# GNN attention over sorted edges: 132 groups of edges summed by counting in place of 120, four in every batch

## The chip, the core and the metric

The kernel runs on one core of a Trainium2 chip. The metric is the device time of one execution in microseconds; the median of three runs of the kernel before is 3422.3 us (3422.07 to 3423.4).

## The reference, cut to what matters

One attention layer of a graph network over 12,500 nodes and 400,000 edges with 64 features each, then a residual and a layer norm. The edges are sorted by destination, and the destinations are drawn as 12500·u², so low nodes have many edges and high nodes few.

```python
z_att = jnp.concatenate([h_src, h_dst, efeats], axis=-1)      # h_src = x[src], h_dst = x[dst]
e = leaky_relu(z_att @ W_attn + b_attn)[:, 0]
m = jnp.concatenate([h_src, efeats], axis=-1) @ W_ne
alpha = softmax of e over the edges of one destination        # segment max, exp, segment sum
z = segment_sum(alpha[:, None] * m, dst)
out = relu(concatenate([x, z]) @ W_out)
return layernorm(x + out)
```

## The kernel before

**Groups and batches.** 512 edges make a group (128 partitions by T = 4); there are 782 groups in the order of the destinations. The first `DG` = 120 groups are *dense*: few nodes receive all their edges. The other 662 are gathered: they go through the main loop in batches of up to 16 groups (`sizes`, from `starts`), in four parts of up to four groups (`lots`); the last four batches have the sizes given by `ENDS` (10, 10, 12 and 6). That makes 43 batches, numbered from 0.

**A gathered group.** GpSimd (POOL) fetches the source rows with four indirect DMAs a group (`gather`, L348, 128 rows of 65 floats each, from `table` to `zx`), 64 for a batch of 16. `scores` (L383 to L409) computes the scores of one part on VectorE (DVE): products and sums with the edge features (L390, L392), the addition of the gathered term (L397, which waits for the part's gathers), the one-hot of the destinations and its sums (L399 to L408). When the four parts of a batch are scored, `softmax` runs on the batch (L721 is its first instruction), then `weights` (L818), and TensorE (PE) multiplies `zx` by the weights (`products`, L835): two parts right after the softmax, two inside the next batch's softmax. `add_in` (L852) adds the sums into `acc`, a ring of 2048 columns with 48 spare columns at its end, which `unwrap` folds back.

**A dense group** needs no gather. Its source terms are looked up by one-hot products (`look_turn`, `look_products`, L470, and `look_scores`, L495 to L501). Rounds of 12 dense groups (`ROUNDS`) join the softmax of a batch. Then `dense_counts` builds, per group, one-hots of source block and node on ScalarE (ACT; L509, L510 and, for nodes above `FIT` = 5, L522, L523), weighted one-hots `lows` on DVE (L512), and multiplies them on PE into a PSUM bank (L517) and, for the sixth and seventh node of a group, into two columns shared by all groups (`more_nodes`, L525). `dense_sum` adds these into `counts` (L535, L538). At the end of a *chunk* of dense groups (`CHUNKS`) `node_products` multiplies `counts` with all of x (L594, 50 instructions on PE), `node_pick` takes the result and clears `counts` (L602, L605, L607), `node_turn` and `node_sum` add it to the sums. `NODS` says how many nodes a group of a given number may span, `EACHS` how many dense groups a batch takes (four below group 84, three from there).

**The order** of instructions is written out by hand for PE, DVE, ACT, SP and POOL (`tc.manual_schedule`): each engine runs what the loop issues, in the loop's order. Per batch, over the parts i = 0 to 3: scores of part i; at i = 0 `node_products` of a chunk that the batch before has closed, then the products with the edges' features (L578), and, after a chunk, `finish3` of a block of nodes that is complete (L1093 to L1109); at i = 1 the first look-up, the first dense group's counts and `between` (`far` on ACT, L664, and on DVE L668, which waits for it); at i = 2 the look-ups' edge scores (L480 to L489) and, only where a batch has four, the second group's counts. Inside the softmax `dense_step(n)`, n = 0 to 3, does `node_pick` (n = 0), the look-ups' scores, `dense_sum`, and the remaining counts (n = 2, 3):

```python
if n == 0 and opened:
    opened = node_pick(*opened)
...
if n in (0, 3):
    while open_counts:
        dense_sum(*open_counts.pop(0))
```

Gathers are kept in step with PE: a gather at a place of a batch waits for a PE instruction (`marks`, `STEPS`), and single-element matmuls (`look_at`, L339) wait on PE for gathers to land; a gather four places on waits for each of them.

The counts' one-hots and the look-ups' share six buffers (`big`, `BIG` = 6). In the batches with looks, the one-hot for the sixth node is written to a buffer that the first look-up's product (L470) must have read.

In the kernel before, chunks from group 84 on have six groups, two batches of three; so every second of these batches has a chunk's `node_products`.

Of the kernel before, what the change touches and what calls it, by code (L numbers as in the profile page):

```python
# [25 lines left out]
S = 48  # L26
# [6 lines left out]
HQ = 4  # L33
EW = 65
ZB = 8
ROUNDS = (12, 12, 12, 12, 12, 12, 12, 12, 12, 12)
DB = len(ROUNDS)
EACHS = ((84, 4), (120, 3))
EACH = max(n for _, n in EACHS)
CHUNKS = ((36, 1), (12, 2), (8, 3), (6, 6))  # L40
NODS = ((16, 2), (36, 3), (60, 4), (87, 5), (108, 6), (120, 7))
FIT = 5
ND = 32
HC = 4
# [3 lines left out]
RING = 2048  # L48
# [10 lines left out]
BF16 = mybir.dt.bfloat16  # L59
# [4 lines left out]
def sorted_path(ctx, tc, x, dst, idx, edge, w_ne, w_attn, b_attn, w_out, out, flag):  # L64
# [6 lines left out]
    nc = tc.nc  # L71
# [19 lines left out]
    ones_col = const.tile([P, 1], F32, name="ones_col")  # L91
    nc.vector.memset(ones_col, 1.0)

    ENDS = ((3, 3, 2, 2), (3, 3, 2, 2), (3, 3, 3, 3), (2, 2, 1, 1))
    sizes = [sum(parts) for parts in ENDS]
    DG = sum(ROUNDS)
    BD = max(ROUNDS)
# [19 lines left out]
    def nodes_of(g):  # L117
        return next(n for upto, n in NODS if g < upto)

# [24 lines left out]
    acc = const.tile([P, RING + S], F32, name="acc")  # L144
# [6 lines left out]
    wins = [dram.tile([P, S], F32, name=f"wins{k}") for k in range((NG + P - 1) // P)]  # L151
# [279 lines left out]
    def look_loads(g0, n):  # L431

        many = nodes_of(g0)
        wrow = tiny.tile([P, EACH, NOD], F32, name="wrow_d", bufs=1)[:, :, 0:many]
        nc.sync.dma_start(out=wrow[:, 0:n], in_=wins[0][g0:g0 + n, 0:many].unsqueeze(0).to_broadcast([P, n, many]))
        return dense_edges(g0, n, "ed", True), wrow

    def look_row(g):
# [89 lines left out]
    def dense_sum(g, to):  # L528

        _, vs = nc.values_load_multi_w_load_instructions(  # L530
            rel[0:1, g:g + 1], engines=(EngineType.DVE,), min_val=0, max_val=ND - nodes_of(g),
            skip_runtime_bounds_check_because=within)
        n = min(FIT, nodes_of(g))
        at = counts[:, :, ds(vs[0], n)]
        nc.vector.tensor_tensor(at, at, to.rearrange("p (h n) -> p h n", n=n), op=OP.add)  # L535
# [62 lines left out]
    def node_pick(g0, pairs):  # L598

        pr = feats.tile([P, SG, T, D], F32, name="pr", bufs=1)  # L600
        mine = pr[:, 0]
        nc.vector.tensor_tensor(mine, pairs[:, 0:HC * D].rearrange("p (h f) -> p h f", f=D),  # L602
                                own.unsqueeze(2).to_broadcast([P, HC, D]), op=OP.mult)
        sums_ = work.tile([P, D], F32, name="sums_", bufs=1)
        nc.vector.tensor_reduce(sums_, mine.rearrange("p h f -> p f h"), axis=AX.X, op=OP.add)  # L605
        if g0 + chunk_sizes[-1] < DG:
            nc.vector.memset(counts, 0.0)  # L607
        return g0, sums_
# [233 lines left out]
    def add_in(g0, n, pg, b0, fac):  # L842
        Sk = widths[starts.index(b0)]
        _, vs = nc.values_load_multi_w_load_instructions(
            column[b0][0:1, g0 - b0:g0 - b0 + n], engines=(EngineType.DVE,), min_val=0, max_val=RING - 1,
            skip_runtime_bounds_check_because=within)
        for g in range(n):
            if g == 0 and fac is not None:
                a1 = acc[:, ds(vs[0], 1)]
                nc.vector.tensor_scalar(a1, a1, fac, None, op0=OP.mult)  # L850
            ag = acc[:, ds(vs[g], Sk)]
            nc.vector.tensor_tensor(ag, ag, pg[:, g, :], op=OP.add)  # L852
# [36 lines left out]
    ids = pre.tile([DG, P, 2 * T], I32, name="ids", bufs=1)  # L889
    nc.sync.dma_start(out=ids, in_=idx[0:DG])  # L890
# [10 lines left out]
    with before:  # L901
# [23 lines left out]
        with tc.manual_schedule(engines={EngineType.DVE, EngineType.Pool, EngineType.Activation, EngineType.PE, EngineType.SP}):  # L925
# [59 lines left out]
            parted_row = pre.tile([DG, P, T], I32, name="parted_row", bufs=1)  # L985
            nc.vector.tensor_scalar(parted_row, ids[:, :, 0:T], P - 1, None, op0=OP.bitwise_and)
            low_row = pre.tile([DG, P, T], BF16, name="low_row", bufs=1)
            nc.scalar.activation(low_row, parted_row, AF.Copy)
            nc.sync.dma_start(out=low_rows, in_=low_row)
# [136 lines left out]
    with loop:  # L1126
# [55 lines left out]
        with tc.manual_schedule(engines={EngineType.PE, EngineType.DVE, EngineType.Activation, EngineType.SP, EngineType.Pool}):  # L1182
# [13 lines left out]
            for k, G in enumerate(sizes):  # L1196
# [22 lines left out]
                for i, (g0, n) in enumerate(lots[k]):  # L1219
# [628 lines left out]
```

## Time and profile before

| | |
|---|---|
| median of three runs | 3422.3 us |
| the profiled execution | 3425.55 us, span 3423.7 us |
| granted TensorE clock, mean | 0.683 |
| busy, share of the span | POOL 73%, PE 67%, DVE 62%, ACT 38% |
| gathers from `table` (L348) | 2584 |
| matmuls of `products` (L835) | 5152, 1059.7 us busy |
| `node_products` (L594) | 600 in 12 chunks, 157.8 us busy |

Busy shares are means over the span; POOL's does not count the time in which it issues. In the text a *lap* is the time from the softmax's first instruction (L721) of one batch to that of the next. A lap has a softmax half (L721 to the first L390 of the next batch's scores) and a scores half (from there to the next L721).

### The profile page before, as it was taken

Reading aid. Unit: us, or ns where it says so; the run is one execution under the profiler, and the core shown is the slowest. Engines: PE = TensorE matmul, PEld = TensorE weight load, DVE = VectorE, ACT = ScalarE, POOL = GpSimd, SP = SyncE. Lnnn points to the kernel's source line nnn. Section 1 sums busy time; section 2 is a strip of 40 time slices with the busy share of each in tenths; the row PEclk is TensorE's granted clock in tenths of the full one; section 3 lists DMA queues with packets and bytes.
Section 4 is the critical chain, followed back from the end, with each engine's and each line's share of the span. In section 5 each row is a group of like instructions: output and inputs, shape, how many; then the busy total and the mean of one; then the engine's idle time right before and its main releaser. Section 6 shows DMA issues by size and latency. Waiting matters only on the chain. (4 is left out here: it accounts for less than half of the span.)

```text
span 3423.7 us, 39637 instructions
## 1 busy us (share of the span) xinstructions
PE 2283.8 (67%) x10338; PEld 1912.0 (56%) x10338; DVE 2121.2 (62%) x5433; ACT 1292.3 (38%) x2838; POOL 2513.9 (73%) x2676
## 2 busy tenths in 40 slices
PE   0244456676677687786878787766767677776844
PEld 0144456666566575665657565655656565554743
DVE  5644455566666676666666666756667675656665
ACT  0211123343343344344444444234444444444321
POOL 6777777777777777777777777777777777777672
PEclk9999995555555566666666676656666676776655
DMA  9433333333333343333333333333333333333231
GB/s 127 87 67 67 67 73 76 74 75 74 78 77 82 75 84 78 85 76 77 79 75 76 71 73 72 77 70 75 75 73 78 71 64 71 66 69 61 46 69 21
DMA packets 518237, 250.75 MB, mean 73 GB/s; under 512 B 354395, under 2 KB 475578, under 8 KB 518003
## 3 DMA queue, kind: packets, MB, share of 16 engines
q1 hardware_dynamic: 429756, 159.38, 20.2%
q0 software_dynamic: 84960, 88.33, 16.4%
q8 instruction: 87, 1.43, 0.2%
q10 hardware_dynamic: 3286, 0.40, 0.2%
q14 instruction: 148, 1.20, 0.1%
HBM read 241.09 MB, written 6.79 MB: 72 GB/s over the span
## 5 line engine op out<-in xcount | busy, mean ns | idle before, releaser
L348 POOL DMA_INDIRECT zx<-table,srcs x2584 | 2443.5, 946 | 826.4 <-issue 697.4
L835 PE MATMUL pg<-w,zx 128*128 128x16 f32 (+9 forms) x5152 | 1059.7, 378 | 14.4 <-DVE w L818 11.9
L835 PEld LDWEIGHTS pg<-w,zx 128*128 128x128 f32 x5152 | 1041.9, 312 | 35.0 <-DVE w L818 13.8
L517 PE MATMUL pg<-big,lows 128*128 128x490 f32 (+3 forms) x960 | 498.0, 682 | 226.0 <-DVE lows L512 223.5
L517 PEld LDWEIGHTS pg<-big,lows 128*128 128x128 f32 x960 | 246.2, 271 | 418.0 <-issue 312.1
L509 ACT ACTIVATE big<-places,place 128x490 f32<-128x490 int16 (+3 forms) x480 | 293.8, 612 | 34.5 <-PE pg L470 33.7
L339 PE MATMUL pps<-zx,ident 1*1 1x1 f32 x272 | 24.4, 159 | 421.2 <-DMA zx<-table,srcs 421.2
L392 DVE TENSOR_REDUCE fixed<-pr 128x16 f32<-128x1024 f32 (+3 forms) x172 | 204.2, 1187 | 162.8 <-ACT fixed L387 154.0
L625 PE MATMUL lines<-ident,bnd 128*1 128x128 f32 x172 | 52.0, 405 | 318.2 <-ACT bnd L728 299.3
L510 ACT ACTIVATE big<-big 128x490 f32<-128x490 f32 (+3 forms) x480 | 257.1, 536 | 15.3
L339 PEld LDWEIGHTS pps<-zx,ident 1*1 1x1 f32 x272 | 10.9, 76 | 448.9 <-DMA zx<-table,srcs 388.6
L470 PE MATMUL pg<-s_src,big 128*128 128x98 f32 x960 | 256.9, 447 | 0.2 <-ACT big L452 0.2
L397 DVE TENSOR_TENSOR fixed<-fixed,zx 128x16 f32<-128x16 f32 (+3 forms) x172 | 31.7, 184 | 363.7 <-DMA zx<-table,srcs 359.3
L470 PEld LDWEIGHTS pg<-s_src,big 128*128 128x128 f32 x960 | 235.4, 329 | 0.9 <-ACT big L452 0.3
L390 DVE TENSOR_TENSOR pr<-ze,lines 128x1024 f32<-128x1024 f32 (+3 forms) x172 | 201.5, 1172 | 8.9 <-DMA ze<-in_edge_dram 8.7
L387 ACT ACTIVATE fixed<-wrow 128x96 f32<-128x96 f32 (+11 forms) x172 | 44.8, 261 | 419.9 <-DVE w L818 143.3
L625 PEld LDWEIGHTS lines<-ident,bnd 128*1 128x1 f32 x172 | 12.8, 97 | 324.8 <-ACT bnd L728 314.1
L723 ACT ACTIVATE soft<-turned 128x128 f32<-128x128 f32 x43 | 16.7, 389 | 459.0 <-DVE turned L721 459.0
L497 DVE TENSOR_TENSOR pr<-pr,pg 128x392 f32<-128x392 f32 x120 | 67.5, 562 | 196.7 <-PE pg L470 195.2
L388 ACT ACTIVATE zx<-ze 128x1024 f32<-128x1024 f32 (+3 forms) x172 | 176.5, 1026 | 11.2 <-DMA zx<-table,srcs 2.3
L852 DVE TENSOR_TENSOR acc<-acc,pg 128x16 f32 (+9 forms) x662 | 123.0, 186 | 77.9 <-issue 19.6
L512 DVE TENSOR_SCALAR lows<-fixed,low,kept 128x128 f32<-128x128 f32 x480 | 163.7, 401 | 8.0 <-PE pg L517 7.6
(305 smaller groups left out, 3010.1 us busy)
## 6 DMA issues: line engine op xcount, KB each, us to landing
ze<-in_edge_dram SPq DMA_DIRECT2D x326, 256.0 KB
zx<-table,srcs POOLq DMA_INDIRECT x2584
low_of<-low_rows SPq DMA_DIRECT2D x120, 128.0 KB
ep<-in_edge_dram SPq DMA_DIRECT2D x120, 128.0 KB
ed<-in_edge_dram SPq DMA_DIRECT2D x54, 256.0 KB
table<-xall SPq DMA_DIRECT2D x7, 455.0 KB
out_dram<-yo SPq DMA_DIRECT2D x24, 128.0 KB
xall<-in_x_dram SPq DMA_DIRECT2D x13, 224.0 KB
```

The costliest lines, as they stand in the source:

```text
L348: issued.append(nc.gpsimd.indirect_dma_start(out=zx[0:r, g, t, 1:EW] if plain else zx[0:r, g, t, 0:EW], out_offset=None, in_=x[:, :] if pl ...
L388: nc.scalar.activation(zx[0:r, 0:n, :, EW:EW + D], ze[0:r, 0:n], AF.Copy)
L390: nc.vector.tensor_tensor(pr[0:r, 0:n], ze[0:r, 0:n], w_edge[0:r].unsqueeze(1).to_broadcast([r, n, T, D]), op=OP.mult)
L392: nc.vector.tensor_reduce(ysum[0:r, 0:n], pr[0:r, 0:n], axis=AX.X, op=OP.add)
L470: at_hand[0] = nc.tensor.matmul(found[:, t, :], hot[:, :, t], s_src, start=True, stop=True).ins
L497: nc.vector.tensor_tensor(hits, hits, found, op=OP.mult)
L509: nc.scalar.activation(hi, places[:, 0:wide], AF.Square, bias=place[:, t, g:g + 1])
L510: nc.scalar.activation(hi, hi, AF.Relu, scale=-1.0, bias=1.0)
L512: nc.vector.tensor_scalar(lows[t], count_, low[:, t, g:g + 1], kept[:, t, kept_at(g):kept_at(g) + 1], op0=OP.is_equal, op1=OP.mult)
L517: at_hand[0] = nc.tensor.matmul(to, lows[t], highs[t], start=(t == 0), stop=(t == T - 1)).ins
L835: at_hand[0] = nc.tensor.matmul(pg[:, g, :], zx[:, g, t, 1:EW + D], w[:, g, t, :], start=(t == 0), stop=(t == T - 1)).ins
L852: nc.vector.tensor_tensor(ag, ag, pg[:, g, :], op=OP.add)
```

## The change

`DG` grows from 120 to 132 (eleven rounds of 12), so 12 groups leave the main loop: 650 groups are gathered, in 42 batches, the last four of 12, 12, 12 and 6. Every batch takes four dense groups. From group 84 on, a chunk is four groups, so that each of these batches closes a chunk; groups from 84 to 107 may span six nodes, those to 131 seven. `node_pick` moves from the softmax's first step to just ahead of the scores of the third part, for all chunks; where the batch's groups span more than five nodes, `dense_sum` of the first group stands behind it, so that the second group's counts find the shared columns free. In `add_in` the ring's spare columns are folded once per batch. Some loads at the start are made in two pieces, since 132 groups exceed 128 partitions.

```diff
-ROUNDS = (12, 12, 12, 12, 12, 12, 12, 12, 12, 12)
+ROUNDS = (12, 12, 12, 12, 12, 12, 12, 12, 12, 12, 12)
-EACHS = ((84, 4), (120, 3))
+EACHS = ((132, 4),)
-CHUNKS = ((36, 1), (12, 2), (8, 3), (6, 6))
-NODS = ((16, 2), (36, 3), (60, 4), (87, 5), (108, 6), (120, 7))
+CHUNKS = ((36, 1), (12, 2), (8, 3), (4, 12))
+NODS = ((16, 2), (36, 3), (60, 4), (84, 5), (108, 6), (132, 7))
...
-    ENDS = ((3, 3, 2, 2), (3, 3, 2, 2), (3, 3, 3, 3), (2, 2, 1, 1))
+    ENDS = ((3, 3, 3, 3), (3, 3, 3, 3), (3, 3, 3, 3), (2, 2, 1, 1))
...
             if g == 0 and fac is not None:
+                nc.vector.tensor_tensor(acc[:, 0:S], acc[:, 0:S], acc[:, RING:RING + S], op=OP.add)
+                nc.vector.memset(acc[:, RING:RING + S], 0.0)
                 a1 = acc[:, ds(vs[0], 1)]
...
+                    if i == 2 and opened:
+                        opened = node_pick(*opened)
+                    if i == 2 and batch_counts and nodes_of(batch_counts[0]) > FIT:
+                        while open_counts:
+                            dense_sum(*open_counts.pop(0))
                     hot = scores(g0, n, tiles[i], drel, b0, k == 0)
...
-                    if n == 0 and opened:
-                        opened = node_pick(*opened)
```

On DVE, in the scores half of the lap that ends with the softmax of batch 29 (a batch with a chunk and with groups of six nodes), ahead of the third part's scores. Before (`far` is what L668 waits for; L390 is the third part's first instruction):

```order
L512 TENSOR_SCALAR lows<-fixed,low,kept 128x128 x4
L668 ISA step,ups<-far 128x129
L668 ISA ups 128x1
L390 TENSOR_TENSOR pr<-ze,lines 128x1024
L392 TENSOR_REDUCE fixed<-pr 128x16
```

And in the changed kernel at the same place:

```order
L512 TENSOR_SCALAR lows<-fixed,low,kept 128x128 x4
L668 ISA step,ups<-far 128x129
L668 ISA ups 128x1
L602 TENSOR_TENSOR pr<-pg,own 128x256
L605 TENSOR_REDUCE sums__17881<-pr 128x64
L607 MEMSET counts 128x3136
L530 TENSOR_LOAD rel
L535 ISA
L535 TENSOR_TENSOR counts<-counts,pg 128x98x5
L538 ISA
L538 TENSOR_TENSOR counts<-counts,pps 128x98
L390 TENSOR_TENSOR pr<-ze,lines 128x1024
```

The chunk's pick and the first group's sums now stand between `far` and the third part's scores.

On PE in the same batch, from `node_products` (L594) to the softmax's first product (L625). Before:

```order
L594 MATMUL pg<-xall,counts 128x256 x24
L594 MATMUL pg<-xall,counts 64x128
L578 MATMUL pg<-wd,ep 128x12 x6
L470 MATMUL pg<-s_src,big 128x98 x4
L517 MATMUL pg<-big,lows 128x490 x4
L525 MATMUL pps<-big,lows 128x98 x4
L339 MATMUL pps<-zx,ident 1x1 x2
L625 MATMUL lines<-ident,bnd 1x4x32 x2
```

And in the changed kernel:

```order
L594 MATMUL pg<-xall,counts 128x256 x24
L594 MATMUL pg<-xall,counts 64x128
L578 MATMUL pg<-wd,ep 128x12 x8
L470 MATMUL pg<-s_src,big 128x98 x4
L517 MATMUL pg<-big,lows 128x490 x4
L525 MATMUL pps<-big,lows 128x98 x4
L517 MATMUL pg<-big,lows 128x490 x4
L525 MATMUL pps<-big,lows 128x98 x4
L339 MATMUL pps<-zx,ident 1x1 x2
L625 MATMUL lines<-ident,bnd 1x4x32 x2
```

A second group's counts (L517, L525) now stand ahead of the two matmuls that wait for gathers, and the products with the edges' features have eight instructions in place of six. This sequence comes in each of batches 26 to 33 (with looks) and, without L470, in batches 34 to 37; before it came in every second one of these batches.

More of the change, by code (lines that the diff above doesn't have):

```diff
@@ L434, in look_loads @@
         wrow = tiny.tile([P, EACH, NOD], F32, name="wrow_d", bufs=1)[:, :, 0:many]
-        nc.sync.dma_start(out=wrow[:, 0:n], in_=wins[0][g0:g0 + n, 0:many].unsqueeze(0).to_broadcast([P, n, many]))
+        nc.sync.dma_start(out=wrow[:, 0:n], in_=wins[g0 // P][g0 % P:g0 % P + n, 0:many].unsqueeze(0).to_broadcast([P, n, many]))
         return dense_edges(g0, n, "ed", True), wrow
@@ L888, in sorted_path @@
     lists[1] = listed(1)
-    ids = pre.tile([DG, P, 2 * T], I32, name="ids", bufs=1)
-    nc.sync.dma_start(out=ids, in_=idx[0:DG])
+    ids = [pre.tile([min(P, DG - a), P, 2 * T], I32, name="ids", bufs=1 + (DG - 1) // P) for a in range(0, DG, P)]
+    for a, part in zip(range(0, DG, P), ids):
+        nc.sync.dma_start(out=part, in_=idx[a:min(a + P, DG)])
     nc.sync.dma_start(out=meet, in_=dst[DG * GE - 1:DG * GE + 1].unsqueeze(0))
@@ L984, in sorted_path @@
             nc.scalar.activation(count_, places[:, 0:P], AF.Copy)
[L985 to L989, printed above, removed]
+            for a, part in zip(range(0, DG, P), ids):
+                n = min(P, DG - a)
+                parted_row = pre.tile([P, P, T], I32, name="parted_row", bufs=1)[0:n]
+                nc.vector.tensor_scalar(parted_row, part[:, :, 0:T], P - 1, None, op0=OP.bitwise_and)
+                low_row = pre.tile([P, P, T], BF16, name="low_row", bufs=1)[0:n]
+                nc.scalar.activation(low_row, parted_row, AF.Copy)
+                nc.sync.dma_start(out=low_rows[a:a + n], in_=low_row)
             of_dense = dense_list()
```

## The prediction

> **What bounds the kernel now.** I read first the groups of instructions and POOL's own line. (Columns of the first row: busy us, mean ns | idle before; of the second: duration min/median/max, first and last start.)
>
> ```profile
> L348 POOL DMA_INDIRECT zx<-table,srcs x2584 | 2443.5, 946 | 826.4 <-issue 697.4 <-DMA zx<-table,srcs 41.5 <-PE pps L339 25.7
> ...
> L348 POOL DMA_INDIRECT zx<-table,srcs x2584: 862/945/3402, 101.0 to 3369.8; - x199
> ```
>
> From 101.0 to 3369.8 us POOL does nothing but gather: 2584 gathers in 3268.8 us, and nearly all of its idle time is called issue, that is, it waited for nothing. Then I cut the time into laps, from one softmax's start to the next, and into stretches of laps. (Columns: length, then busy us and instructions of PE, PEld, DVE, ACT and POOL, then the granted clock.)
>
> ```profile
> 1793.80:1873.80 80.00, 70.14 (x297) 55.64 (x297) 54.11 (x139) 39.11 (x76) 60.48 (x65) 0.71 0.38 79
> 2113.60:2765.70 652.10, 462.29 (x2120) 381.24 (x2120) 423.58 (x1025) 269.70 (x568) 486.43 (x515) 0.65 0.35 73
> 2353.80:2436.60 82.80, 62.86 (x301) 52.16 (x301) 52.53 (x130) 37.74 (x79) 62.68 (x67) 0.73 0.34 72
> 2436.60:2517.50 80.90, 56.31 (x261) 46.08 (x261) 57.11 (x135) 38.02 (x81) 58.69 (x63) 0.63 0.37 76
> 2765.70:3088.50 322.80, 232.99 (x1102) 187.62 (x1102) 203.28 (x492) 150.25 (x340) 239.98 (x254) 0.67 0.33 66
> 3088.50:3345.70 257.20, 164.98 (x806) 140.02 (x806) 155.40 (x403) 94.99 (x225) 181.15 (x192) 0.61 0.30 59
> ```
>
> A lap of 64 gathers takes 80.0 us where nothing else interferes (first row), so a gather costs 80.0 / 64 = 1.25 us. No other engine is near full. But the lap 2353.80 to 2436.60 takes 82.8: it scores a batch with a chunk of six-node groups. Its DVE tells why.
>
> ```profile
> 2391.66 1.22 DVE L390 TENSOR_TENSOR pr<-ze,lines 128x1024 f32<-128x1024 f32 x1
> ...
> 2412.38 1.36 DVE L512 TENSOR_SCALAR lows<-fixed,low,kept 128x128 f32<-128x128 f32 x4
> 2422.54 0.29 DVE L668 CUSTOM_DVE_ANT_0 step<-far 128x129 f32<-128x129 f32 x1 [8.81 <-ACT far L664]
> ...
> 2422.76 1.21 DVE L390 TENSOR_TENSOR pr<-ze,lines 128x1024 f32<-128x1024 f32 x1
> ...
> 2433.80 0.19 DVE L397 TENSOR_TENSOR fixed<-fixed,zx 128x16 f32<-128x16 f32 x1
> ...
> 2436.61 0.32 DVE L721 STREAM_TRANSPOSE turned<-soft 128x128 f32<-128x128 f32 x1
> ```
>
> DVE idles 8.81 us ahead of the third part, for `far` on ACT. At 2433.80 L397, which waits for the part's gathers, does not wait at all: here the gathers are not the bound, the chain PE, ACT, DVE is. The two engines ahead of it:
>
> ```profile
> 2403.27 13.68 PE L594 MATMUL pg<-xall,counts 128*128 128x256 f32 x50 [4.17 <-DVE earlies L1275]
> 2416.88 1.51 PE L578 MATMUL pg<-wd,ep 128*128 128x12 f32 x12
> 2418.24 2.08 PE L470 MATMUL pg<-s_src,big 128*128 128x98 f32 x8
> 2420.16 3.48 PE L517 MATMUL pg<-big,lows 128*128 128x490 f32 x8
> 2423.48 1.03 PE L525 MATMUL pps<-big,lows 128*128 128x98 f32 x8
> ...
> 2420.36 1.18 ACT L522 ACTIVATE big<-places,place 128x98 f32<-128x98 int16 x4 [7.73 <-PE pg L470]
> ...
> 2422.22 0.30 ACT L664 ACTIVATE far<-edges_of 128x130 f32<-128x130 int32 x1
> ```
>
> PE runs the chunk's products for 13.68 us, then the edge products and the first look-up (L470). ACT's L522 wants the buffer that L470 reads, waits 7.73 us, and `far` stands behind it on ACT.
>
> **The change part by part.** All terms stand against this execution, 3425.55 us with a span of 3423.7; it is 3.3 above the median of 3422.3, to which I add the sum.
>
> *Gathers removed.* 12 groups of four: 48 × 1.25 = −60.0 us, as long as POOL is what the lap waits for.
>
> *Late laps with looks: eight laps, 2113.60 to 2765.70 before.* Now each of them scores a batch with a chunk, four six- or seven-node groups and four looks. Two things stand on DVE behind `far` that were in the softmax half. Their rows, with the pick's and the sums' place in the softmax half of a chunk's batch:
>
> ```profile
> 2436.61 0.32 DVE L721 STREAM_TRANSPOSE turned<-soft 128x128 f32<-128x128 f32 x1
> ...
> 2438.59 0.41 DVE L602 TENSOR_TENSOR pr<-pg,own 128x256 f32<-128x256 f32 x1
> ...
> 2440.22 2.67 DVE L607 MEMSET counts<- 128x3136 f32 x1 [0.60 <-issue]
> ...
> 2445.98 0.67 DVE L535 TENSOR_TENSOR counts<-counts,pg 128x490 f32 x1 [0.34 <-issue]
> ...
> 2449.18 0.56 DVE L497 TENSOR_TENSOR pr<-pr,pg 128x392 f32<-128x392 f32 x1 [1.24 <-PE pg L470]
> ...
> 2457.72 1.36 DVE L512 TENSOR_SCALAR lows<-fixed,low,kept 128x128 f32<-128x128 f32 x4
> ...
> 2472.26 0.74 DVE L818 TENSOR_TENSOR w<-hot,fixed 128x576 f32<-128x576 bf16 x1
> ```
>
> Scores half: it was 2436.61 − 2391.66 = 44.95. The pick adds 2440.22 + 2.67 − 2438.59 = 4.3; the first group's sums 1.4 (issue 0.34, L535 0.67, and about half of that for the sixth node); the second group's `lows`, now ahead of the fourth part, 1.36; the look-ups' edge scores for four groups in place of three some 0.6 (estimate: a third more of L480 and L481, about 1 us each); four more edge matmuls on PE ahead of `far`, 0.5 (a third of 1.51). Together 8.2: 53.1. Nothing behind `far` waits, so nothing there can swallow it. Softmax half: the pick's 4.3 us leave, but at 2449.18 DVE waits for PE's L470, which starts from the softmax, not from the pick; DVE would only wait longer: gain 0. The fourth look's scores add four DVE instructions, three like L497's 0.56 and a short one, 1.9; a fourth group's weights 0.4 (estimate). The half in which the chunk's softmax ran began at 2436.61; its weights (L818) at 2472.26 are followed by four of these and 4.2 us later by the next scores, 39.9 in all; now 42.2. Lap: 53.1 + 42.2 = 95.3.
>
> Off that: two of the eight have no `finish3` ahead of `node_products`, which saves the 4.17 us for which L594 waited there, 1.0 in the mean; the first lap starts with a lead of some 4, 0.5 in the mean; and PE, with shorter pauses, may run its softmax products at a higher clock. The same 32 instructions take:
>
> ```profile
> 2474.26 4.52 PE L835 MATMUL pg<-w,zx 128*128 128x36 f32 x32
> ...
> 2478.90 7.04 PE L835 MATMUL pg<-w,zx 128*128 128x36 f32 x32
> ```
>
> 2.5 us apart, and two such products' worth lies on the softmax's path, so 0 to 5; I take half, 2.5. The mean is 95.3 − 4.0 = 91.3, say 91: 8 × 91 = 728 against 652.1, **+76**. Ends: 86 a lap (all the clock, some overlap that I do not see), +36; 96, +116.
>
> *Late laps without looks: four, 2765.70 to 3088.50.* Here `far` is early and the pick waits for L594:
>
> ```profile
> 3047.01 1.22 DVE L390 TENSOR_TENSOR pr<-ze,lines 128x1024 f32<-128x1024 f32 x1
> ...
> 3057.49 12.56 PE L594 MATMUL pg<-xall,counts 128*128 128x256 f32 x50 [2.67 <-DVE earlies L1275]
> ...
> 3085.30 0.18 DVE L397 TENSOR_TENSOR fixed<-fixed,zx 128x16 f32<-128x16 f32 x1 [7.24 <-DMA zx<-table,srcs]
> ```
>
> L594 ends 23.0 us after the scores began; the sums then wait for PE's L578, L517 and twice L525 (7.0 by the rows above), and end at 31.5. Two parts and one `lows` follow, each part some 5.9: 44.6. With a softmax half of 38.3 + 0.4 that is 83.3, and the first of the four still has the looks' softmax half, 87: 337 against 322.8, **+14** (0 to +25).
>
> *Five earlier chunks.* The pick moves for them too. In the first such lap:
>
> ```profile
> 1200.74 12.52 PE L594 MATMUL pg<-xall,counts 128*128 128x256 f32 x50
> ...
> 1207.33 1.21 DVE L390 TENSOR_TENSOR pr<-ze,lines 128x1024 f32<-128x1024 f32 x1
> ...
> 1223.99 0.18 PE L339 MATMUL pps<-zx,ident 1*1 1x1 f32 x2
> ...
> 1225.94 0.18 DVE L397 TENSOR_TENSOR fixed<-fixed,zx 128x16 f32<-128x16 f32 x1 [2.85 <-DMA zx<-table,srcs]
> ```
>
> The third part would start at 1213.26 + 4.3 instead of 1207.33, 10.2 later; 2.85 of it is free at L397, and shorter waits for PE and ACT give back about 3.5. What is left, some 4, reaches POOL through L339, behind the delayed counts. 5 × 4 = **+20** (0 to +35).
>
> *Tail, 3088.50 to 3345.70.* 192 gathers would take 240; it took 257.2. Three batches of 12 now follow a full one, and its lap of 38.5 + about 37 meets 60 us of gathers; with a lead of 5 it loses 11, the rest some 3: **−3** (−12 to +8).
>
> *Front, folds, loads.* A fold is two short DVE instructions per batch ahead of `far`'s wait, and elsewhere ahead of waits for gathers: 0; without that cover 0.3 × 41 = 12. The second load of indices lies beside the first gathers: 0, at most 2.
>
> Sum: −60 + 76 + 14 + 20 − 3 = **+47**: 3472.5 for a profiled execution, **3469** against the median. A measurement of this kernel tells about 0.2%, 7 us, from no change.
>
> **The rivals.**
>
> *The gathers remain the bound* (faster). If the pick and the sums hide behind something, the eight late laps stay near the 82.8 of the lap above: 8 × 82 = 656, +4; the other late laps and the early chunks 0. −60 + 4 − 3 = −59: 3363. For it: DVE is busy only 52.53 of that lap's 82.80. Against: the pick stands behind L668, not in its wait. It decides below 84 a lap. Chance 0.13.
>
> *PE warms up* (about the same, or faster). The granted clock is 0.73 in the lap with a chunk to multiply and 0.63 in the next. If the denser late laps hold PE near its full clock, the two softmax products lose the whole 5 us and `far` comes 3 earlier (estimate: a fifth off L594's 13.68): 86 a lap, +36; without looks +6; early +5; −60 + 36 + 6 + 5 − 3 = −16: 3406. Chance 0.14. The Trainium skill, "TensorE: Matmul & The Clock Gate", Part 1, says that the array's clock is at half by default and at full after about 3.4 us of sustained activity, which speaks for this rival; by that rule alone the eight laps would stand at 86. The 4.52 and 7.04 us above agree with a ratio somewhat below two.
>
> *More piles up* (slower still). The second count's one-hots on ACT delay the fourth part's copies, or each pick waits for PE as well: 97 a lap and 8 per early chunk: −60 + 124 + 25 + 40 + 5 = +134 at worst, in the middle about +95: 3517. Chance 0.07.
>
> That fewer groups are gathered than said is no rival: the order has 2532 + 4 gathers from `table` in place of 2580 + 4.
>
> **How the numbers follow.** The forecast, 3469, has 0.66; its own range is 3425 to 3510. The range for 8 in 10 reaches down over the warm-clock case, 3400, and up to 3515. Faster by over 0.2%: 0.13 of the first rival and 0.09 of the second, 0.22. Within 0.2%: 0.02 of the forecast and 0.03 of the second rival, 0.05. Slower: the rest, 0.73.
>
> **What would show it.** Right: laps of about 91 us from batch 25's softmax to batch 33's, with L397 waiting for no gather there, L668 idle for 8 to 12 us for `far` in each, and POOL held by L339; L602 waiting for PE in the early chunks. Wrong: late laps of 80 to 83 with waits at L397, or L668 not waiting. Lap lengths between 84 and 88 with a clock above 0.8 would speak for the warm PE.

## The result, and the profile after

| | before | changed |
|---|---|---|
| median, same chip | 3422.2 us (3417.3 to 3423.4, 4 runs) | 3484.1 us (3479.0 to 3484.7, 4 runs) |
| ratio, 95% interval | | 1.018 (1.0168 to 1.0192) |
| the profiled execution | 3425.55 us | 3483.85 us |

The change costs 61.9 us by the medians and 58.3 by the two profiled executions; 47 were forecast. The runs below were made on two other chips, on which the kernel before took 3420 to 3423 us, and three of them on a chip on which it took 4014 us (the slow chip); those three can be compared only with the kernel before on that chip.

In the changed kernel, lines from 849 on have moved down by two (`add_in`) to ten (`earlies`, L1285); the lines of PE's, ACT's and POOL's steps named here kept their numbers. First the stretches of the kernel before that are not shown above (length, then busy us and instructions of PE, PEld, DVE, ACT and POOL, then clock):

```profile
1148.50:2113.60 965.10, 756.42 (x3122) 606.21 (x3122) 645.83 (x1658) 425.64 (x866) 725.70 (x769) 0.66 0.38 77
...
3088.50:3423.70 335.20, 202.71 (x1204) 172.26 (x1204) 197.69 (x543) 111.86 (x269) 200.01 (x212) 0.59 0.25 49
```

And the same view of the changed kernel, cut at the softmax of batches 13, 25, 33 and 37, and one late lap:

```profile
0.00:1144.80 1144.80, 634.76 (x2806) 567.12 (x2806) 661.59 (x1753) 339.59 (x803) 862.00 (x927) 0.75 0.39 80
1144.80:2144.40 999.60, 770.81 (x3146) 619.19 (x3146) 659.93 (x1695) 430.77 (x874) 725.78 (x769) 0.65 0.33 76
2144.40:2874.30 729.90, 574.86 (x2649) 463.78 (x2649) 498.00 (x1200) 365.18 (x777) 480.63 (x510) 0.73 0.31 70
2874.30:3216.30 342.00, 281.97 (x1325) 223.40 (x1326) 226.76 (x546) 187.77 (x432) 241.18 (x256) 0.74 0.28 62
3216.30:3482.10 265.80, 161.20 (x1008) 142.67 (x1007) 157.20 (x448) 78.45 (x188) 158.40 (x168) 0.57 0.23 49
2410.40:2502.20 91.80, 71.73 (x333) 57.84 (x332) 63.11 (x158) 46.38 (x99) 60.37 (x64) 0.74 0.31 70
```

| stretch | before | changed | difference | forecast |
|---|---|---|---|---|
| to the softmax of batch 13 | 1148.5 | 1144.8 | −3.7 | 0 |
| laps 13 to 24 (five early chunks) | 965.1 | 999.6 | **+34.5** | +20 |
| laps 25 to 32 (chunk and looks) | 652.1 | 729.9 | **+77.8** | +76 |
| laps 33 to 36 (chunk, no looks) | 322.8 | 342.0 | **+19.2** | +14 |
| the rest, with one batch and 48 gathers fewer | 335.2 | 265.8 | **−69.4** | −63 |

The late lap from 2410.40 to 2502.20 (lap 28, the one that starts with the softmax of batch 28) in the timeline of DVE (start, duration):

```profile
2451.91 1.22 DVE L390 TENSOR_TENSOR pr<-ze,lines 128x1024 f32<-128x1024 f32 x1
...
2481.11 0.29 DVE L668 CUSTOM_DVE_ANT_0 step<-far 128x129 f32<-128x129 f32 x1 [8.55 <-ACT far L664]
...
2481.32 0.42 DVE L602 TENSOR_TENSOR pr<-pg,own 128x256 f32<-128x256 f32 x1
...
2482.97 2.67 DVE L607 MEMSET counts<- 128x3136 f32 x1 [0.60 <-issue]
2485.75 0.67 DVE L535 TENSOR_TENSOR counts<-counts,pg 128x490 f32 x1
...
2495.54 1.36 DVE L512 TENSOR_SCALAR lows<-fixed,low,kept 128x128 f32<-128x128 f32 x4
...
2499.39 0.18 DVE L397 TENSOR_TENSOR fixed<-fixed,zx 128x16 f32<-128x16 f32 x1
```

`far` is waited for as before, 8.55 us. Behind it now stand the pick (2481.32 to 2485.64, 4.3 us), the first group's sums and, at 2495.54, the second group's `lows`; L397 waits for no gather. The softmax half is 41.5 us and the scores half 50.3. PE and ACT in the same lap:

```profile
2413.24 5.40 PE L835 MATMUL pg<-w,zx 128*128 128x36 f32 x32
...
2449.24 3.99 PE L835 MATMUL pg<-w,zx 128*128 128x36 f32 x32
...
2453.35 7.04 PE L835 MATMUL pg<-w,zx 128*128 128x36 f32 x32
...
2462.00 13.07 PE L594 MATMUL pg<-xall,counts 128*128 128x256 f32 x50 [1.60 <-DVE earlies L1285]
...
2476.80 2.08 PE L470 MATMUL pg<-s_src,big 128*128 128x98 f32 x8
2478.72 3.48 PE L517 MATMUL pg<-big,lows 128*128 128x490 f32 x8
...
2496.09 5.67 PE L517 MATMUL pg<-big,lows 128*128 128x490 f32 x8 [13.02 <-DVE lows L512]
```

```profile
2478.93 1.18 ACT L522 ACTIVATE big<-places,place 128x98 f32<-128x98 int16 x4 [7.56 <-PE pg L470]
...
2480.78 0.30 ACT L664 ACTIVATE far<-edges_of 128x130 f32<-128x130 int32 x1
```

The chain is the one of the kernel before (L594, L470, L522, `far`), now in every lap. PE's second count waits 13.02 us for DVE. The early laps look different. DVE and PE in lap 13, from 1144.8 to 1226.7, and POOL behind laps 13, 16, 19, 21 and 23, the five that hold an early chunk's products:

```profile
1208.47 0.42 DVE L602 TENSOR_TENSOR pr<-pg,own 128x256 f32<-128x256 f32 x1 [10.43 <-PE pg L594]
...
1212.72 1.16 DVE L390 TENSOR_TENSOR pr<-ze,lines 128x1024 f32<-128x1024 f32 x1
```

```profile
1221.23 5.56 PE L517 MATMUL pg<-big,lows 128*128 128x392 f32 x8 [6.32 <-DVE lows L512]
1226.73 0.23 PE L339 MATMUL pps<-zx,ident 1*1 1x1 f32 x4
```

```profile
1227.65 0.94 POOL L348 DMA_INDIRECT zx<-table,srcs  x1 [6.92 <-ACT soft L723]
...
1474.37 0.94 POOL L348 DMA_INDIRECT zx<-table,srcs  x1 [5.70 <-issue]
...
1723.82 0.95 POOL L348 DMA_INDIRECT zx<-table,srcs  x1 [8.65 <-ACT soft L723]
...
1891.20 0.95 POOL L348 DMA_INDIRECT zx<-table,srcs  x1 [7.83 <-ACT soft L723]
...
2058.83 0.94 POOL L348 DMA_INDIRECT zx<-table,srcs  x1 [6.61 <-issue]
```

The pick waits 10.43 us for L594, the third part starts at 1212.72, the second count ends late, and L339, which stands behind it, lets POOL go on only at 1227.65: 6.92 us without a gather. (The row names ACT as the releaser; by the program this gather waits for a look at L339, which ran at 1226.73.) The trace bears the program out: from the softmax of batch 13 to that of batch 33 POOL has 13 pauses of over 5 us, and every one of them ends 0.7 us behind a group of L339, whatever releaser its row names. Eight of them stand at the ends of the eight late laps with looks, one at each (6.3 to 17.2 us). The other five are the rows above, 35.7 us. Less the 0.30 us that POOL takes ahead of an ordinary gather, they come to 34.2, as good as all of the 34.5 us that laps 13 to 24 lost; in the kernel before, POOL's longest pause there is 2.75 us.

### The profile page after: what moved, and what is told of

The parts are those of the page before. It is cut to its first block, busy times and chain, and to the rows that moved or that the text cites. A ratio compares the mean times of both kernels' runs of the same rounds, so it can differ in the third digit from the quotient of the medians.

```text
span 3482.1 us, 41374 instructions
## 1 busy us (share of the span) xinstructions
PE 2423.6 (70%) x10932; PEld 2016.2 (58%) x10932; DVE 2203.5 (63%) x5640; ACT 1401.8 (40%) x3074; POOL 2468.0 (71%) x2628
## 5 line engine op out<-in xcount | busy, mean ns | idle before, releaser
L348 POOL DMA_INDIRECT zx<-table,srcs x2536 | 2397.3, 945 | 935.8 <-issue 669.9
L835 PE MATMUL pg<-w,zx 128*128 128x20 f32 (+9 forms) x5056 | 1031.0, 376 | 17.7 <-DVE w L818 17.7
L835 PEld LDWEIGHTS pg<-w,zx 128*128 128x128 f32 x5056 | 1013.6, 309 | 38.0 <-DVE w L818 17.5
L517 PE MATMUL pg<-big,lows 128*128 128x490 f32 (+3 forms) x1056 | 554.5, 687 | 375.3 <-DVE lows L512 367.3
L517 PEld LDWEIGHTS pg<-big,lows 128*128 128x128 f32 x1056 | 269.7, 270 | 590.2 <-issue 500.9
L509 ACT ACTIVATE big<-places,place 128x490 f32<-128x490 int16 (+3 forms) x528 | 326.7, 619 | 49.8 <-PE pg L470 39.7
L392 DVE TENSOR_REDUCE fixed<-pr 128x16 f32<-128x1024 f32 (+2 forms) x168 | 200.3, 1193 | 145.5 <-ACT fixed L387 134.5
L470 PE MATMUL pg<-s_src,big 128*128 128x98 f32 x1056 | 283.3, 447 | 0.8 <-ACT big L452 0.8
L470 PEld LDWEIGHTS pg<-s_src,big 128*128 128x128 f32 x1056 | 259.0, 329 | 1.8 <-ACT big L452 0.9
L594 PE MATMUL pg<-xall,counts 128*128 128x256 f32 x900 | 234.4, 426 | 25.0 <-DVE earlies L1285 20.7
L625 PE MATMUL lines<-ident,bnd 128*1 128x128 f32 x168 | 48.4, 388 | 262.5 <-ACT bnd L728 258.9
L594 PEld LDWEIGHTS pg<-xall,counts 128*128 128x128 f32 x900 | 192.9, 218 | 64.2 <-issue 31.9
L387 ACT ACTIVATE fixed<-wrow 128x144 f32<-128x144 f32 (+9 forms) x168 | 44.0, 262 | 430.8 <-DVE lows L512 159.5
L390 DVE TENSOR_TENSOR pr<-ze,lines 128x1024 f32<-128x1024 f32 (+2 forms) x168 | 197.4, 1175 | 6.3 <-DMA ze<-in_edge_dram 6.1
L397 DVE TENSOR_TENSOR fixed<-fixed,zx 128x16 f32<-128x16 f32 (+2 forms) x168 | 31.0, 185 | 260.6 <-DMA zx<-table,srcs 256.0
L339 PE MATMUL pps<-zx,ident 1*1 1x1 f32 x212 | 17.4, 159 | 234.6 <-DMA zx<-table,srcs 234.5
L388 ACT ACTIVATE zx<-ze 128x1024 f32<-128x1024 f32 (+2 forms) x168 | 173.1, 1030 | 10.3 <-DMA zx<-table,srcs 1.4
L451 ACT ACTIVATE big<-low_of,p_col 128x512 f32<-128x512 bf16 x132 | 94.2, 713 | 193.8 <-DMA low_of<-low_rows 193.4
L854 DVE TENSOR_TENSOR acc<-acc,pg 128x24 f32 (+9 forms) x650 | 121.0, 186 | 76.6 <-issue 20.5
```

The lines of the kernel that those rows point to most:

```text
L348: issued.append(nc.gpsimd.indirect_dma_start(out=zx[0:r, g, t, 1:EW] if plain else zx[0:r, g, t, 0:EW], out_offset=None, in_=x[:, :] if pl ...
L388: nc.scalar.activation(zx[0:r, 0:n, :, EW:EW + D], ze[0:r, 0:n], AF.Copy)
L390: nc.vector.tensor_tensor(pr[0:r, 0:n], ze[0:r, 0:n], w_edge[0:r].unsqueeze(1).to_broadcast([r, n, T, D]), op=OP.mult)
L392: nc.vector.tensor_reduce(ysum[0:r, 0:n], pr[0:r, 0:n], axis=AX.X, op=OP.add)
L470: at_hand[0] = nc.tensor.matmul(found[:, t, :], hot[:, :, t], s_src, start=True, stop=True).ins
L509: nc.scalar.activation(hi, places[:, 0:wide], AF.Square, bias=place[:, t, g:g + 1])
```

## The experiments

The first seven kernels below and the one with only 120 groups ran on one chip, with the kernel before at 3419.8 to 3420.6 us. The changed kernel itself was not run there: its 3484 stands against 3422.2 on its own chip, so that differences to it are good to about 2 us. Stretches are cut as in the table above.

**The early pick put back.**

```diff
-                    if i == 2 and opened:
+                    if i == 2 and opened and (not batch_counts or nodes_of(batch_counts[0]) > FIT):
                         opened = node_pick(*opened)
...
+                    if n == 0 and opened and batch_counts and nodes_of(batch_counts[0]) <= FIT:
+                        opened = node_pick(*opened)
```

> The changed kernel with one part undone: where the batch's groups span up to five nodes, the pick is back in the softmax's first step (five early chunks); late batches are as changed. Theory: the pick ahead of the third part delays the second group's counts, and through the look at L339 the next batch's gathers; undone it gives back the 34.5 us that laps 13 to 24 lost against before: 3450, laps 13, 16, 19, 21, 23 without the long wait of POOL. The prediction's own size of that term, 20: 3464. Rival: the early laps lost their time to something else (the folds of the ring, the sums' place): no change, 3484.

Measured: 3463.7 us (ratio 1.0132, 1.0116 to 1.0149). Laps 13 to 24 and lap 17 alone, in the windows of this kernel:

```profile
1145.10:2124.10 979.00, 756.34 (x3146) 611.18 (x3146) 659.24 (x1695) 429.50 (x874) 725.16 (x769) 0.65 0.34 77
...
1466.20:1550.80 84.60, 59.90 (x251) 48.09 (x251) 57.59 (x147) 36.42 (x74) 60.35 (x65) 0.60 0.33 75
```

The stretch goes from 999.6 to 979.0, 20.6 less, and 13.9 more than before are left, so that the run's first theory misses. But these 13.9 us are not a rest of what the changed kernel lost: POOL's five pauses are all gone. What is left stands in laps 17, 22 and 24 (84.6 here, 85.4 and 85.9), in which a `finish3` falls into a lap that now also holds a pick. In the changed kernel these laps hold a `finish3` but no pick, which stands one lap earlier there. So putting the pick back takes one loss away and brings a smaller one in.

**The finishes one batch later.** A block of nodes is finished in the batch after the one at which `starts` reaches its share of the edges. With 12 groups fewer to gather, `starts` is higher by 12 in every batch, so that some blocks come due one batch earlier: the seven in question at batches 14, 16, 18, 20, 21, 23 and 24 in place of 14, 17, 18, 20, 22, 24 and 25 (from `need` and `starts`), each finished in the lap that follows.

```diff
         due[k].append(c0)
+    for k in (24, 23, 21, 16):
+        due[k + 1], due[k] = due[k], []
```

> The changed kernel with the early chunks' pick back in the softmax (run before, 3464), and with the finish of four node blocks one batch later (due 16, 21, 23, 24 become 17, 22, 24, 25). Theory: of the 34.5 that laps 13 to 24 lost, 14 are laps 17, 22 and 24 (84.6, 85.4, 85.9), in which a finish3 now falls into the lap of a pick; before, no finish did, since blocks come due at other batches when 12 groups fewer are gathered. One batch later, two of the finishes stand in laps with a chunk's products, where they cost nothing, and one in a lap of its own (82): -12, 3452. Rival: those laps are long for the folds and the moved widths: no change, 3464.

Measured: 3450.3 us (1.0087, 1.0069 to 1.0105), 13.4 less than with the early pick alone. The windows of this kernel:

```profile
1144.00:2108.90 964.90, 759.92 (x3130) 614.33 (x3130) 656.86 (x1688) 425.49 (x867) 725.27 (x769) 0.65 0.35 78
```

964.9 against 965.1 before: with the pick back in the softmax, the meeting of pick and finish costs 14.1 us, and once it is gone nothing is left. This does not make the finishes a second part of the changed kernel's 34.5 us: the kernel with only 120 groups, further down, has its finishes where they were before and the pick ahead of the third part, and loses more there, not less.

**`far` ahead.** `between` goes ahead of the look-up's and the counts' one-hots on ACT, and so of L522, which waits there. The edit does this in every batch; it is meant for the late laps.

```diff
                     if k and i == 1 and (batch_looks or batch_counts or joined is not None):
                         add_up()
+                    if i == (0 if final else 1):
+                        if more:
+                            as_floats(k + 2, lists[k + 2])
+                        if k + 1 < len(sizes):
+                            after = between(k + 1)
```

> The changed kernel with between (far on ACT, L668 on DVE) moved ahead of the first look-up's one-hots and the first group's counts. Theory: far stands behind L522 on ACT, which waits for the buffer that L470 reads; moved ahead of it, L668 no longer waits, and DVE waits for L594's end at the pick instead, some 5.6 earlier; the sums behind it then wait for the first group's L525, so that 2.5 of it is left per late lap with looks: -20, 3464, and L668's 8 to 12 us of idle time are gone. Rival: the wait is PE's products (L594, then L470, L517, L525) whatever is ahead on ACT: L668's wait turns up at L602 and L535 in full, 3484. Second rival: far ahead of the one-hots delays the look-up on ACT: slower, 3490.

Measured: 3461.8 us (1.0124, 1.0108 to 1.0141). What DVE waited for in laps 25 to 32 (us in total, times, longest), in the changed kernel and in this one:

```profile
DVE step L668 <- ACT far L664: 78.1, 8, 12.0
...
DVE counts L535 <- PE pg L517: 25.0, 8, 3.8
```

```profile
DVE counts L535 <- PE pg L517: 49.9, 16, 3.8
...
DVE pr L602 <- PE pg L594: 22.1, 8, 5.8
```

The wait for `far`, 78.1 us, is gone, and 47 of it come back, 22.1 at the pick (for L594) and 24.9 more at the sums (for L517). These eight laps take 702.1, 3.5 less each, against 2.5 expected; laps 13 to 24, where DVE never waited more than 1.3 us for `far`, lose 6.5. The chain PE, ACT, `far` is real, but right behind it stands PE alone.

**Without the clear of `counts`.** The price of DVE's work behind `far`. This kernel leaves the clear out from group 84 on, so that its sums are wrong; only its time is of use.

```diff
-        if g0 + chunk_sizes[-1] < DG:
+        if g0 + chunk_sizes[-1] < DG and g0 + chunk_sizes[-1] < 84:
             nc.vector.memset(counts, 0.0)
```

> The changed kernel without the clearing of counts (L607, 2.67 us on DVE) in the eleven chunks from group 84 on; their sums are left wrong. Theory: DVE is on the path behind far, so each clear counts in full in the laps with looks (8 x 2.67 = 21) and is hidden by the sums' wait for PE in the laps without: 3463; if it counts in all eleven, 3455. Rival: gathers or PE set the late laps, and DVE has room: 3484.

Measured: 3465.9 us (1.0132, 1.0115 to 1.0149), 18 less. Laps 25 to 32 and 33 to 36 in its windows:

```profile
2144.30:2854.30 710.00, 574.07 (x2645) 462.37 (x2645) 478.72 (x1193) 365.22 (x777) 479.81 (x509) 0.74 0.32 72
2854.30:3196.10 341.80, 278.56 (x1331) 220.72 (x1331) 215.90 (x542) 187.79 (x432) 241.57 (x256) 0.75 0.28 62
```

The eight laps are 19.9 us shorter; the first of them still clears, so that is 7 × 2.67 = 18.7 and a little more: there DVE is on the path. Lap by lap it is uneven: laps 26 and 27 gain 0.7 and 0.8, laps 28 to 32 gain 3.1 to 5.3, so that the agreement with the clear's own length holds in the sum alone. The four laps without looks are 0.2 shorter: there the sums wait for PE anyway. Both as this run's theory had it.

**Pick and second count in the softmax.**

```diff
-                    if i == 2 and opened:
-                        opened = node_pick(*opened)
...
+                    if n == 0 and opened:
+                        opened = node_pick(*opened)
...
+                    if n == 1 and many_ and len(batch_counts) > 3:
+                        open_counts.append(dense_counts(batch_counts[1]))
```

(`many_`: the groups span over five nodes; then the sums are also taken at n = 2.)

> The changed kernel with the pick back in the softmax's first step everywhere, and, where groups span over five nodes, the second group's counts moved from the third part into the softmax's second step (its sums ahead of the third's counts). Theory: what stands behind far on DVE (pick 4.3, sums 1.4, lows 1.4) is what made the late laps long. Without it the scores half is some 46 in place of 53, and the softmax half takes a part of it back (a fourth group's lows and sums, up to 2, and PE's counts): 88 a lap with looks in place of 91 (-24), 82 without looks in place of 85.5 (-14), early chunks -34: 3412. Rival: four groups in a lap are simply more work, wherever it stands: only the early chunks gain, 3450.

Measured: 3445.9 us (1.0076, 1.006 to 1.0093), nearer to the rival. Its windows:

```profile
1145.70:2121.60 975.90, 750.59 (x3146) 608.51 (x3146) 659.53 (x1694) 429.70 (x874) 725.16 (x769) 0.66 0.34 77
2121.60:2836.90 715.30, 563.20 (x2625) 455.61 (x2625) 490.49 (x1191) 356.53 (x759) 487.05 (x517) 0.73 0.32 72
```

The eight laps gain 14.6 in place of 24. In the lap of batch 29 the scores half falls from 49.0 to 41.5 and the softmax half rises from 40.0 to 44.0. Its first wait in these laps is still

```profile
DVE step L668 <- ACT far L664: 76.1, 8, 11.2
```

A likely reading, which no run tests by itself: the waits for PE in the softmax half, which had hidden one pick in every second batch, hide only a part of a pick and a fourth group in each.

**Both together, and with the finishes.** `far` goes ahead only where groups span over five nodes.

```diff
+                    if i == 1 and not final and bool(batch_counts) and nodes_of(batch_counts[0]) > FIT:
+                        if more:
+                            as_floats(k + 2, lists[k + 2])
+                        if k + 1 < len(sizes):
+                            after = between(k + 1)
```

> The kernel with the pick in the softmax and the second group's counts in its second step (run before, 3446), with between moved ahead of the first look-up in batches whose groups span over five nodes. Theory: its late laps' scores half (44.9 with 30.6 of DVE busy) is set by L668's wait for far, 8 to 11 us behind L522; nothing else there waits for PE, so the whole wait goes, down to what gathers set: eight laps of 89.4 become about 82: -55, 3390, and the waits for gathers at L397 come back. Rival: far is only one of several things that PE's products hold (copies on ACT behind L522, L339 behind the counts): the wait moves to the third part's sums, and 3 us per lap are won, 3422.

> Pick and second counts in the softmax, far ahead of the look-up in late batches, and the four finishes one batch later. The three causes stand in different laps, so the gains should add up: 3446 less 55 less 12, 3379; by the rival of the run before, 3410. Both are under the kernel before (3420 to 3422).

Measured: 3431.7 us (1.0037, 1.0025 to 1.0048) and 3424.3 (1.001, 1.0 to 1.002). Not 3390 and 3379: the first one's late laps gain 14.1 where 55 were expected, and its waits in them begin with

```profile
DVE fixed L392 <- ACT fixed L387: 74.0, 16, 9.7
DVE counts L535 <- PE pg L517: 26.1, 12, 3.7
```

where the kernel with `far` behind L522 had 76.1 us of waiting for `far`. The wait has only changed its name: L387, the copy for the third part's scores, stands behind the same one-hots on ACT. In the timeline of ACT and DVE, with all three repairs:

```profile
2343.76 0.70 ACT L451 ACTIVATE big<-low_of,p_col 128x512 f32<-128x512 bf16 x1
...
2350.73 1.18 ACT L522 ACTIVATE big<-places,place 128x98 f32<-128x98 int16 x4 [0.64 <-PE pg L470]
...
2352.37 0.28 ACT L387 ACTIVATE fixed<-wrow 128x144 f32<-128x144 f32 x1
```

```profile
2352.68 1.23 DVE L392 TENSOR_REDUCE fixed<-pr 128x16 f32<-128x1024 f32 x1 [7.80 <-ACT fixed L387]
```

**The copies ahead too.** `copy_in` issues L387 and L388 of the third part, which its `scores` then leaves out.

```diff
+                    if i == 1 and not final and batch_counts and nodes_of(batch_counts[0]) > FIT:
+                        g2, n2 = lots[k][2]
+                        copy_in(g2, n2, tiles[2], b0, *fetched[g2])
                     if k and i < min(2, len(batch_looks)):
                         turns.append(look_turn(rows_ahead.pop(0)))
```

> The kernel with three repairs (run before, 3424), and in late batches the third part's two copies on ACT (L387, L388) moved ahead of the look-up's and the counts' one-hots. Theory: after far was moved, DVE waits 7.8 us in each late lap at L392 for L387, which stands behind the one-hots and L522 on ACT; with the copies ahead that wait goes, and about half of it reaches the lap before the gathers (80 a lap) and PE's chain come in: twelve laps by 3.5, 3382, with waits for gathers at L397. Rival: POOL, held by PE's L339 behind the counts (7 to 13 us in these laps), sets them already: 3424, the wait moves to L397.

> The kernel of copies_ahead once more. That run and its two neighbours fell on a chip on which every kernel, the one before too, took some 17% longer (4014 in place of 3421), with waits of all engines for no named releaser; its ratio to the kernel before was 0.991. Theory, unchanged: on a chip like the first, the wait of 7.8 us at L392 goes and about half of it reaches the lap: 3382; by the ratio 3390. Rival: POOL, held by PE's L339, sets the late laps already: 3424.

Measured: on the slow chip 3976.6 against 4014.5 (0.991, 0.9888 to 0.9932); on a chip like the first 3402.5 against 3423.4 (0.9937, 0.9924 to 0.9951). This version is faster than the kernel before, by 0.6 to 0.9%, and so than the changed one. It gains 21.8 over the three repairs (run on another chip), about half of what was expected. Laps 25 to 32 (lines above are ten further down in this kernel: L407 is L397, L845 is L835, L527 is L517), DVE's first wait there, and POOL's longest for PE:

```profile
2112.70:2794.70 682.00, 561.58 (x2641) 452.99 (x2641) 493.21 (x1197) 360.60 (x766) 484.14 (x513) 0.75 0.34 75
```

```profile
DVE fixed L407 <- DMA zx<-table,srcs: 30.2, 8, 7.0
```

```profile
POOL zx L348 <- PE pg L845: 26.9, 20, 3.4
POOL zx L348 <- PE pg L527: 19.3, 18, 3.4
```

DVE waits for gathers again, and POOL for places in PE's line. So at 85.2 a lap the limit is no longer a queue on ACT, but by these waits PE's pace, with which the gathers are kept in step; no run tested that.

**The kernel before with the same two moves** (`far` and the copies ahead in late batches).

```diff
+                            after = between(k + 1)
...
+                        copy_in(g2, n2, tiles[2], b0, *fetched[g2])
```

> The kernel before with the two moves that concern its order in late batches (between ahead of the look-up, the third part's copies ahead of the one-hots). Theory: its late laps with looks lie 12 us over what gathers set in all (652.1 against 8 x 80), and only every second one closes a chunk, so at most 12 are to be had: 3410 to 3418. Rival: the waits behind L522 cost the kernel before as much per chunk as they cost the changed one: 3395.

Measured, on the slow chip only: 4041.2 against 4014.5 (1.0068, 1.005 to 1.0087). No gain, and a loss that neither theory had. On a chip like the first it was not run, so how much of the gain above belongs to the 132 groups and how much to the two moves stays open.

**Only 120 groups.**

```diff
-ROUNDS = (12, 12, 12, 12, 12, 12, 12, 12, 12, 12, 12)
-EACHS = ((132, 4),)
+ROUNDS = (12, 12, 12, 12, 12, 12, 12, 12, 12, 12)
+EACHS = ((120, 4),)
```

(with nine chunks of four, the node limits cut at 120, and the last batches as before)

> The changed kernel with 120 groups in place of 132 (four in every batch, chunks of four from group 84 on and the pick ahead of the third part, as changed; gathers and the last batches as before). Theory: the cost lies in the laps that close a chunk, the 12 groups only take gathers off: against the changed kernel 48 gathers come back (+60), and three of the eight late laps with looks (91) become laps that gathers set (80), -33: 3511. Rival: the 12 groups themselves (their seven nodes, the shorter main loop) cost what was lost: about the time of before, 3420 to 3440.

Measured: 3498.5 us (1.0224, 1.0206 to 1.0243). The rival falls: the new order costs 78 us where not one group fewer is gathered. Laps 13 to 24 and then laps 34 to 36, the last chunk's and the two behind it, with 196 gathers:

```profile
1142.50:2150.10 1007.60, 783.97 (x3146) 621.03 (x3146) 657.62 (x1694) 430.77 (x874) 724.99 (x769) 0.64 0.33 75
...
2935.70:3182.30 246.60, 132.38 (x659) 117.32 (x659) 127.07 (x292) 64.57 (x145) 184.84 (x196) 0.57 0.29 61
```

The last three laps take 1.26 us a gather: gathers set them. Laps 13 to 24 lose 42.5 us against the kernel before. In this kernel the finishes fall into the same laps there as before (13, 15, 18, 19, 21 and 23, by their instructions in the trace), and only the pick's place and the fold of the ring are new. So with the pick ahead of the third part the finishes' move did not cost the changed kernel anything: it lost 8.0 us less with it (the two kernels differ there also in which edges a batch holds).

The 12 groups themselves gain 14 of their 60. Against this kernel, the profiled execution of the changed one is 52.1 us shorter from the softmax of batch 37 on and 8.0 in laps 13 to 24, but 39.7 longer in laps 25 to 36. Most of that is in laps 31 and 32 (95.8 and 97.9 in place of 81.8 and 86.2), which have looks only because of the 12 groups.

**Without the fold.**

```diff
-                nc.vector.tensor_tensor(acc[:, 0:S], acc[:, 0:S], acc[:, RING:RING + S], op=OP.add)
-                nc.vector.memset(acc[:, RING:RING + S], 0.0)
```

> The changed kernel without the fold of the ring's spare columns in add_in (two short DVE instructions, 41 times). The forecast put them at 0 with 12 as the end without cover. Theory: in nearly all laps they stand ahead of a wait: 3480 to 3484. Rival: in the late laps, which DVE helps to set, they count in full: 3478; everywhere: 3472.

Measured on the slow chip: 4166.6 against 4014.5 (1.0402, 1.037 to 1.0433). The changed kernel was not run there, so this settles nothing. That laps 13 to 24 are back at the length of before with the folds in them (964.9, `finish_later`) puts the fold's price there at about nothing; in the late laps it stays open.

## Why the prediction held, and where it was off

*Gathers and tail*: −63 forecast, −69.4 in the rest and −3.7 ahead of batch 13. Right in kind; the tail had a little more to give, and these 10 us hide a good part of what the early chunks and the laps without looks cost beyond their terms. That the total comes within 15 us of the forecast by the medians is in part luck.

*Late laps with looks*: right, in size and mechanism. 91.2 a lap against 91 forecast; `far` waited for in all eight, no wait for gathers, and POOL held by L339 at the end of each lap. The halves also fit, once the deduction of 4.0 is put where its parts belong: 53.1 − 1.5 = 51.6 for the scores half and 42.2 − 2.5 = 39.7 for the softmax half, against means of 51.2 and 40.1. The 2.5 for the clock was worked out from the softmax's two products, which still took 3.99 and 7.04 us in lap 28; what got faster are the products at the lap's start, 5.40 us in place of 7.04. So that part is in part luck. Taking the clear away showed that DVE's steps behind `far` count there, in the sum at their full length.

*Late laps without looks*: +19.2 against +14, within the stated end of 25. The mechanism (sums waiting for PE) is borne out by the clear, which was free to take away there.

*Early chunks*: +34.5 against +20, just inside the stated end of 35. The mechanism was right (the delayed second count, L339 behind it, POOL standing), and the term was sized too small: 5.7 to 8.7 us of pause at each of the five chunks in place of 4. The delay of the third part itself was about as forecast, 9.1 us in lap 13 against 10.2. What failed is the 2.85 + 3.5 us that were to be given back on the way to L339: it came 6.5 us later in lap 13 and 6.5 to 8.8 in the five laps. A term that the sum did not have is part of it. The second count now stands behind an idle PE and ran at a granted clock of 0.50 to 0.61 in these laps, so that the two counts took 8.4 to 10.9 us together in place of 6.8 to 7.6. How the rest divides was not traced. That `early_back` gave back 20.6, the very figure of the forecast, is luck: that kernel has a new loss of its own in it, and with the finishes where they were before the pick's place costs 42.5. Nor was the prediction's first reading right that no other engine was near full: PE was busy for 70.14 of the 80.00 us of the lap that it shows.

*The rivals*: "the gathers remain the bound" is refuted by L397, which waits for no gather in laps 25 to 32. "PE warms up" came true in part: the granted clock rose from 0.65 to 0.73 in these laps and the products at a lap's start got faster, but the second of the softmax's two products stayed at 7.04 us in lap 28, and the laps stayed at 91. "More piles up" came true only in laps 31 and 32 (95.8 and 97.9), the two with looks in which seven-node groups are counted.

## What to carry to other kernels

When a step is delayed, follow the delay to the instruction that lets the bounding engine go on (here L339, for POOL), and be slow to count on waits that give some of it back. When a size changes, work through every schedule that is derived from it, and ask which periodic steps now fall into the same lap: a pick and a finish that were free apart cost some 5 us together once the pick was put back. So a repair can bring in a loss of its own: what it gives back is not the price of what it undoes, and the pauses in the changed kernel's own trace tell that price better. When a queue is in order and its head waits, name all that stands behind it: moving `far` alone uncovered a copy behind the same instructions (76 us of waiting became 74 at another line), and moving that too took another 22.7 us off eight laps. Work that is hidden in one of two laps has a place to hide; put it in every lap and only a part of it still does.

## What the runs showed of the hardware

PE's same eight matmuls for a count took 3.48 us right behind other products and 5.67 after 13.02 us of idle time, in one lap; the granted clock was 1.00 in the first and 0.62 in the mean of the second, within which it rose. In lap 13 eight smaller ones took 2.82 us at a granted clock of 1.00 and 5.56 at 0.50, after 6.32 us of idle time. The Trainium skill ("TensorE: Matmul & The Clock Gate", Part 1) says that the array's clock is at half by default and at full after sustained activity; the trace agrees, with close to a factor of two where the clock stayed at 0.50.

The slow chip ran the gathers no slower. The kernel before with the two moves had there, among the groups and among POOL's waits:

```profile
L348 POOL DMA_INDIRECT zx<-table,srcs x2584 | 2445.8, 947 | 1434.6 <-issue 720.0
```

```profile
POOL zx L348 <- remote: 270.7, 102, 5.6
```

One gather is busy for 947 ns as on the first chip (946), but POOL's idle time is 1434.6 us in place of the 826.4 of the kernel before on the first chip; 270.7 of it was ended by nothing in the program (`remote`), in pieces of up to 5.6 us. What held the engines there stays open.
